# A four-stage graph network: the first stage's edge network moved into the pass that sorts the edges

## The chip, the cores and the metric

One core of a Trainium2 chip runs the whole program in one launch. The metric is the device time of that launch in microseconds (us). The core has five engines with queues of their own: PE (TensorE, matrix products into PSUM), DVE (VectorE), ACT (ScalarE), POOL (GpSimd, here mostly the issuer of indirect transfers) and SP (SyncE, issuer of plain transfers). ACT's queue issues some transfers too. Each queue is worked off in order, and semaphores join them.

## What is computed

There are 6250 nodes with 48 features (H) and 200000 edges with ends src and dst, sorted by dst. Each edge has 40 numbers for the first stage (`edge_attr_40`, RBF = 40), 16 for the second and a distance (`edge_weight`). Four graph stages follow one another, each with a residual and a layer norm. Only the first part of the first stage is touched by the change:

```python
gate = jax.nn.silu(edge_attr @ F1W + F1b) @ F2W + F2b          # 40 -> 48 -> 48, per edge
ei, ej = emb[atom_z[src]], emb[atom_z[dst]]
gate = gate + (ei * (ej @ adapt)).sum(-1, keepdims=True)       # one number per edge (G = 32)
cw = jnp.where(distances < CUT, 0.5 * (jnp.cos(jnp.pi * distances / CUT) + 1.0), 0.0)
mj = node_mult[dst]
msg = gate * h[dst] * (cw * mj)[:, None]
agg = segment_sum(msg, src); tot = clip(segment_sum(mj, src), 1e-08)
h = _ln(h + agg / tot[:, None], gn, bn)
for i in range(4):                                             # attention layers
    score = (qi * kj).sum(-1) + 0.1 * (edge_attr * qi[:, :40]).sum(-1) + logm[dst]
    ...
```

The later stages (an edge network with sums by dst, and two weighted sums) are the same in both kernels.

## The kernel before

**Layout.** The edges are padded to 200192 = 128 partitions x J columns, J = 1564; partition p holds 1564 consecutive edges. Work on edges goes by groups of columns. Sums over the edges of a node are made by sorting the edges by that node and running a segmented scan (DVE) along each partition.

**Counting, 0 to 535 us.** To sort by src, the kernel finds the place of each edge. `counted` (L311) builds one-hot tiles of the low and the high digit of src per column on DVE (`one_hots`, L304 and L307) and multiplies them on PE into a histogram of 128 x 49 counts, in NS = 4 streams (L317: column b goes to stream b mod 4). `places` adds up the streams. Beside this, `early` (L628 on) runs small steps between the columns: a search for where each dst begins, `node_table` (a row of 81 numbers per node: 48 features times multiplicity, 32 numbers of the type, the multiplicity), the scatter of these rows into `seed` at the first edge of each dst, and products of weights.

**The scatter pass, 535 to 3150 us.** It goes by chunks of CS = 16 columns, 98 of them. Four pieces of code are interleaved by the loop at the end of `sort`, which the tile framework then schedules:

- `ranked` (L366) gives the place `pos` of every edge, 8 columns at a time. Per 4 columns, ACT copies the running counts from PSUM (`hs_ps`) to `hs` (L385), PE looks the counts up (`g`, L387) and adds the 4 columns to `hs_ps` (L389), and only then can the next copy run. DVE makes the one-hot tiles (L304, L307, L380), compares the edges within a column (L395) and picks the result (L398, L400).
- `payload` (L415) loads 16 columns of the edges' attributes and copies them with src, dst and distance into a row tile `r_s` (three buffers), on ACT (L422 to L425).
- `expanded` (L660) fills the last 81 numbers of each row from `seed`: a load, then three slices of 27 features, each with a copy to PSUM on ACT (`run_v`, L287), a scan on DVE (`xf`, L270) and a copy into `r_s` on ACT (L676).
- `beside` does the same as `payload` for the rows that stay sorted by dst (`r_d`), clears tables and scatters a node table.

The main loop has POOL scatter each column of `r_s` to its place in `rows_s` (L172): 1564 indirect transfers, each of 128 rows of WS = 124 numbers (496 bytes). The program runs `ranked` four groups and `payload` one chunk ahead of the scatters.

**The gated sums, 3150 to 4347 us.** `gated_sums` reads the sorted rows back in groups of 40 columns. Per group, `begun` loads the rows `r` and the src-side type rows `q`, works out the cutoff on 128x40 tiles (L915 to L923, with a Sine on ACT, L920), multiplies the 48 features by it on POOL (L924), spreads q along the segments (L287, L270), forms the one number per edge that the types add to the gate (L931, L933) and writes `ra` (the 40 attributes and that number) to `rows_a`. The network itself is a skewed chain over four pairs of columns at a time: PE transposes `ra` (L954), ACT copies (L956), PE multiplies by F1W (L963; two extra rows carry the added number through), ACT applies Silu (L965), DVE copies the two extra rows (L966), PE multiplies by F2W (L973), and DVE multiplies by the features (`v`, L975). Then DVE scans the 49 sums (L986), ACT transposes them into `st` (L989) and writes them out.

**After that.** `between` joins the sums to the nodes (to 4505 us). The four attention layers (to 14060 us) read `rows_a` per 40 columns and gather 40 rows per group on POOL. The edge network (to 17180 us) and the two weighted passes (to 21800 us) follow.

Of the kernel before, what the change touches and what calls it, by code (L numbers as in the profile page):

```python
# [19 lines left out]
P = 128  # L20
N, E, H = 6250, 200000, 48
NB = 49
# [23 lines left out]
def gnn_kernel(ctx: ExitStack, tc: tile.TileContext, A, out: bass.AP):  # L46
# [78 lines left out]
    RA = RBF + 1  # L125
    f1w = const.tile([2 * RA, 2 * H + 2], F32, name="f1w")
    V.memset(f1w, 0.0)
    f1b = const.tile([2 * H, 1], F32, name="f1b")
    f2 = const.tile([2 * H + 3, 2, H], F32, name="f2")
    V.memset(f2, 0.0)  # L130
    for t in range(2):
        nc.sync.dma_start(f1w[t * RA:t * RA + RBF, t * H:(t + 1) * H], A["L0_gnn_F1W"])
        nc.sync.dma_start(f1w[t * RA + RBF:(t + 1) * RA, 2 * H + t:2 * H + t + 1], ones_pp[0:1, 0:1])
        nc.sync.dma_start(f1b[t * H:(t + 1) * H, :], A["L0_gnn_F1b"].rearrange("(w o) -> w o", o=1))
        nc.sync.dma_start(f2[t * H:(t + 1) * H, t, :], A["L0_gnn_F2W"])
        nc.sync.dma_start(f2[2 * H + t:2 * H + t + 1, t, :], ones_pp[0:1, 0:H])
        nc.sync.dma_start(f2[2 * H + 2:2 * H + 3, t, :], A["L0_gnn_F2b"].rearrange("(o w) -> o w", o=1))
# [4 lines left out]

    W0 = H + G + 1
    WS, WD = 3 + RBF + W0, 3 + EF
    rows_a = dram.tile([EP, RA], F32, name="rows_a")
# [153 lines left out]
    NS = 4  # L299
# [11 lines left out]
    def counted(pool, hist, rows_, lo, hi, ns, B):  # L311

        for j0 in range(0, J, B):
            n = min(B, J - j0)
            ol, oh = one_hots(pool, rows_, lo, hi, j0, n, B)
            for b in range(n):
                T.matmul(hist[:, b % ns, :NB], ol[:, b, :], oh[:, b, :],  # L317
                         start=(j0 + b < ns), stop=(j0 + b >= J - ns))
            yield

    def places(k, pool, psum, hist, ns, bases):

        of = pool.tile([P, ns, NB], F32, name="of")
        V.tensor_copy(of, hist[:, :, :NB])
# [41 lines left out]
    def ranked(k, pool, big, psum, consts, lo, hi, key, keyrow, lorow, bases, pos):  # L366

        B = 8
        hs_ps = psum.tile([P, NS, NB], F32, name="hs_ps", bufs=1)
        T.matmul(hs_ps, ident, bases, start=True, stop=True)  # L370
        for j0 in range(0, J, B):
# [11 lines left out]
            for b0 in range(0, n, NS):  # L383
                hs = big.tile([P, NS, NB], F32, name="hs")
                tc.keep_in_program_order(S.copy(hs, hs_ps[:, :, :NB]))  # L385
                for b in range(NS):
                    T.matmul(g[:, b0 + b, :], olt[:, b0 + b, :], hs[:, b, :], start=True, stop=True)  # L387
                for b in range(NS):
                    T.matmul(hs_ps[:, b, :NB], ol[:, b0 + b, :], oh[:, b0 + b, :], start=False, stop=True,  # L389
                             skip_group_check=True)  # L390
# [6 lines left out]
            pick = big.tile([P, B, NB], F32, name="pick")[:, :n, :]  # L397
# [17 lines left out]
    def payload(pool, k, j0, attr, ends, ew):  # L415
# [3 lines left out]
        a = by_columns(pool, wid, attr.shape[1], f"a_{k}", CS)  # L419
        tc.keep_in_program_order(nc.sync.dma_start(a, pj(attr)[:, s, :]))  # L420
        r = by_columns(pool, wid, rows[k].shape[1], f"r_{k}", CS, bufs=3)
        tc.keep_in_program_order(S.copy(r[:, :, 3:3 + attr.shape[1]], a))  # L422
        S.copy(r[:, :, 0], ends[k][:, s])
        S.copy(r[:, :, 1], ends["d" if k == "s" else "s"][:, s])
        S.copy(r[:, :, 2], ew[:, s])  # L425
        return r

    def sort(k, attr, ends, ew, early=None, behind=None, more=None, beside=None):
# [3 lines left out]
        with tc.tile_pool(name=f"sort_{k}", bufs=1) as sp:  # L432
# [3 lines left out]
            with tc.tile_pool(name=f"sort_hist_{k}", bufs=1) as hp, \  # L436
# [13 lines left out]
                hist = psum.tile([P, NS, 512], F32, name="hist")  # L450
# [17 lines left out]
            with tc.tile_pool(name=f"sort_io_{k}", bufs=2) as io, \  # L468
# [7 lines left out]
                rest = more(io, psum2) if more else lambda j0, r: None  # L476
# [21 lines left out]
    fall_i = ends_pool.tile([P, 1], I32, name="fall_i")  # L498
    nsd = ends_pool.tile([P, J], F32, name="nsd")
    logm = const.tile([P, NB], F32, name="logm")  # L500
    t0 = ends_pool.tile([P, NB, W0], F32, name="t0")
# [82 lines left out]
    def node_table(pool, psum):  # L584
# [5 lines left out]
        nc.sync.dma_start(both[:, 0], A["L0_gnn_emb"])  # L590
# [8 lines left out]
        for b0 in range(0, NB, 7):  # L599
            yield  # L600
            z = pool.tile([P, 7, P], I32, name="types", bufs=2)
            nc.sync.dma_start(z, bass.AP(tensor=types.tensor, offset=types.offset + b0 * P, ap=[[0, P], [1, 7 * P]]))
# [24 lines left out]

    def early(pool, hp, psum):  # L628
# [8 lines left out]
        for _ in range(22):  # L637
            yield
        next(search)
        yield from node_table(hp, psum)  # L640
        for _ in range(18):
            yield
# [3 lines left out]
        weight_products(psum)  # L646

# [12 lines left out]
    def expanded(pool, psum):  # L660

        fac = factors(pool, "fac", SG, CS)
# [702 lines left out]
```

## Time and profile before

| | us |
|---|---|
| runs | 21802.45, 21820.60, 21820.88; median 21820.6 |
| profiled execution | 21803.16, of which the span is 21801.4 |
| busy in the span: PE, DVE, ACT, POOL | 5648.7, 8101.9, 4776.3, 13861.4 |
| mean granted TensorE clock | 0.621 of full speed |

One execution was profiled; times of single instructions come from it. In the profile's groups a line reads: source line, engine, operation, output<-inputs, shapes, count | busy us, mean ns of one | idle time of the engine just before these instructions, and what released it. In the timeline a line reads: start, duration, engine, source line, operation, with the idle time before it and its releaser in brackets. "issue" is time in which the engine waited for nothing that the profile shows; "remote" is a release whose source the profile can't name.

### The profile page before, as it was taken

What the parts mean: (1) busy time and instruction counts of PE and PEld (TensorE: products, weight loads), DVE (VectorE), ACT (ScalarE), POOL (GpSimd) and SP (SyncE); (2) the same over time, 40 slices, a digit from 0 to 9 for tenths busy, and PEclk for the clock granted to TensorE, in tenths of its full rate; (3) what the DMA queues carried; (4) which work ended last, traced back from release to release, by engine and by line L of the source; (5) the groups of instructions that cost most, each with busy time, mean ns of one, the idle gap of its engine ahead of it and who ended that gap; (6) DMA issues with size and microseconds to landing.
All of it is one profiled execution on the core that took longest, in us unless ns stands there. A gap on an engine that the chain in (4) does not pass through costs nothing.

```text
span 21801.4 us, 86436 instructions
## 1 busy us (share of the span) xinstructions
PE 5648.7 (26%) x19138; PEld 3381.8 (16%) x19138; DVE 8101.9 (37%) x16477; ACT 4776.3 (22%) x6603; POOL 13861.4 (64%) x13410
## 2 busy tenths in 40 slices
PE   2332337622222222222222222244544200000000
PEld 2332334410001000110001000133333100000000
DVE  6554557743343434333433343322222211110001
ACT  0332334411111111111111111133333200001111
POOL 2566651177776777677776777644444577777777
PEclk9999995555555555555555555566666655555555
DMA  5455444422222222232222222211111111111111
GB/s 156 160 168 135 163 165 180 168 79 86 85 88 65 88 85 88 65 88 85 88 82 70 86 88 86 59 41 43 43 45 44 34 36 34 36 36 36 36 36 36
DMA packets 873557, 1792.31 MB, mean 82 GB/s; under 512 B 365490, under 2 KB 546658, under 8 KB 868034
## 3 DMA queue, kind: packets, MB, share of 16 engines
q1 hardware_dynamic: 349038, 860.63, 12.1%
q0 software_dynamic: 427520, 547.67, 10.9%
q10 hardware_dynamic: 96468, 378.32, 4.6%
q8 instruction: 163, 2.67, 0.1%
q14 instruction: 368, 3.01, 0.0%
HBM read 1144.48 MB, written 641.17 MB: 82 GB/s over the span
## 4 chain that ended last, share of the span: by engine, by line
POOL 29%; issue 13%; PE 6%; another core or an unknown queue 4%; DVE 3%; ACT 2%; DMA 0%; ACTq 0%; POOLq 0%; DVEq 0%; SPq 0%
POOL t L167 28%; PE ps L1216 2%; PE ps L1223 2%; PE ps L1231 2%; POOL own L167 1%; PE ps_t L1209 1%; ACT run_v L287 1%; ACT st L1239 1%; DVE qf L270 1%; DVE sf L270 1%; DVE run_v L268 0%; DVE q L1134 0%; DMA t<-tab_x,other 0%; ACT at L1211 0%
## 5 line engine op out<-in xcount | busy, mean ns | idle before, releaser
L167 POOL DMA_INDIRECT t<-tab_kv,other x6256 | 6586.8, 1053 | 2117.7 <-issue 2075.2
L167 POOL DMA_INDIRECT t<-tab_x,other x4692 | 4787.2, 1020 | 2619.5 <-issue 1459.6
L1132 PE MATMUL ka<-t,ident 128*128 128x480 f32 (+2 forms) x1264 | 1209.1, 1060 | 6818.1 <-DMA t<-tab_kv,other 5869.4
L172 POOL DMA_INDIRECT rows_s<-r_s,scratch x1564 | 1524.8, 975 | 1032.8 <-ACT r_s L422 528.6
L1134 DVE TENSOR_TENSOR q<-qf,ka 128x480 f32<-128x480 f32 (+2 forms) x632 | 676.6, 1074 | 3791.7 <-issue 3146.9
L1132 PEld LDWEIGHTS ka<-t,ident 128*128 128x128 f32 x1264 | 316.8, 310 | 7533.7 <-issue 4066.5
L270 DVE TENSOR_TENSOR_SCAN qf<-fac,run_v 128x480 f32<-128x480 f32 (+1 forms) x943 | 1028.8, 1092 | 672.1 <-DVE run_v L268 357.1
L841 PE MATMUL cy_ps<-ident,last_s 128*48 128x128 f32 (+1 forms) x4 | 1.6, 405 | 4524.6 <-DVE last_s L276 4524.6
L1164 ACT COPY st<-m 128x40 f32<-128x40 f32 (+3 forms) x164 | 42.8, 261 | 4895.8 <-DVE sc L1137 3754.0
L387 PE MATMUL g<-hs,olt 128*128 128x49 f32 x3128 | 758.7, 417 | 1323.0 <-ACT hs L385 764.4
L287 ACT COPY run_v<-q 128x480 f32<-128x480 f32 (+1 forms) x943 | 851.8, 916 | 707.7 <-DMA q<-spread_s 258.6
L1133 PE MATMUL ka<-r,tenth 128*128 128x400 f32 (+2 forms) x1264 | 954.6, 858 | 0.0
L1225 DVE TENSOR_SCALAR h<-ps,b 128x512 f32<-128x512 f32 x391 | 293.6, 751 | 1710.6 <-PE ps L1216 902.9
L387 PEld LDWEIGHTS g<-hs,olt 128*128 128x128 f32 x3128 | 695.9, 327 | 1375.5 <-ACT hs L385 791.9
L1313 DVE TENSOR_TENSOR run_v<-t,w_ps 128x480 f32<-128x480 f32 (+3 forms) x164 | 142.1, 912 | 1832.9 <-DMA t<-tab_x,other 1832.9
L268 DVE SCALAR_TENSOR_TENSOR run_v<-last_s,ns,run_v 128x12 f32<-128x12 f32 x480 | 98.0, 219 | 1935.4 <-issue 1680.1
L924 POOL TENSOR_TENSOR r<-r,u 128x1920 f32<-128x1920 f32 (+3 forms) x41 | 135.5, 3305 | 1037.0 <-DVE u L923 958.7
L270 DVE TENSOR_TENSOR_SCAN sf<-dec,run_v 128x480 f32<-128x480 f32 (+5 forms) x820 | 731.3, 922 | 122.3 <-remote 57.1
L841 PEld LDWEIGHTS cy_ps<-ident,last_s 128*48 128x48 f32 (+1 forms) x4 | 0.5, 127 | 4525.3 <-ACT st L1319 2261.5
L1216 PE MATMUL ps<-at,w 112*128 112x512 f32 x782 | 535.7, 774 | 496.2 <-ACT h L1218 471.7
L1163 ACT COPY st<-sf 128x1960 f32<-128x1960 f32 (+3 forms) x164 | 621.1, 3787 | 44.9 <-DVE sf L270 25.1
L1156 DVE TENSOR_TENSOR run_v<-t,es 128x480 f32<-128x480 f32 (+2 forms) x656 | 616.7, 962 | 13.9 <-DVE sf L270 5.3
(395 smaller groups left out, 14775.8 us busy)
## 6 DMA issues: line engine op xcount, KB each, us to landing
q<-spread_s SPq DMA_DIRECT2D x190, 960.0 KB
state_a<-st ACTq DMA_DIRECT2D x152, 1000.0 KB
r<-rows_a SPq DMA_DIRECT2D x152, 820.0 KB
state_h<-st ACTq DMA_DIRECT2D x114, 960.0 KB
t<-tab_kv,other POOLq DMA_INDIRECT x6256
r<-rows_s SPq DMA_DIRECT2D x38, 2480.0 KB
t<-tab_x,other POOLq DMA_INDIRECT x4692
seed<-zeros SPq DMA_DIRECT2D x17, 3726.0 KB
```

Source lines behind the costliest of these rows:

```text
L167: return nc.gpsimd.indirect_dma_start(out=dst, out_offset=None, in_=table, in_offset=bass.IndirectOffsetOnAxis(ap=idx, axis=0))
L172: i = nc.gpsimd.indirect_dma_start(out=table, out_offset=bass.IndirectOffsetOnAxis(ap=idx, axis=0), in_=src, in_offset=None)
L270: V.tensor_tensor_scan(flat[:, f0 * wid:(f0 + n) * wid], fac[:, :n * wid], v.rearrange("p f c -> p (f c)")[:, :n * wid], 0.0, OP.mult, OP.add)
L287: return lambda v, f0, n: S.copy(v, by_feature(src[:, :, f0:f0 + n]))
L387: T.matmul(g[:, b0 + b, :], olt[:, b0 + b, :], hs[:, b, :], start=True, stop=True)
L1132: T.matmul(ka, ident, t[:, j0:j1, 0:H], start=True, stop=False)
L1133: T.matmul(ka[:, :, 0:RBF], tenth, r[:, j0:j1, 0:RBF], start=False, stop=True)
L1134: V.tensor_mul(q[:, j0:j1, :], by_column(qf)[:, j0:j1, :], ka)
L1156: V.tensor_mul(v, by_feature(t[:, :, H + 1 + f0:H + 1 + f0 + n]), es[:, None, :].to_broadcast([P, n, wid]))
L1163: S.copy(st[:, :, 0:H + 1], by_column(sf))
L1216: T.matmul(ps, w1, at, start=True, stop=True)
L1223: T.matmul(ps, w2, h1, start=True, stop=True)
```

## The change

- A second, transposed copy of `edge_attr_40` (`edge_attr_40_t`: 80 rows, two columns' attributes, by 782 x 128) becomes an input. From it, per 16-column chunk, the first layer and Silu run in the scatter pass a chunk ahead (`hidden`, in four tiles `hid0` to `hid3`), and the second layer runs when the chunk's rows are filled; ACT copies its result from PSUM into `r_s`.
- A row of `rows_s` grows from 124 to 172 numbers (688 bytes): attributes first, then src, dst, the cutoff in place of the distance, 48 gate numbers, and the 81 from `seed`.
- NS goes from 4 to 8: `hs` is copied once per 8 columns. `hist` takes one PSUM bank, and its streams start from a zero product.
- `cutoff` works out all 128x1564 cutoffs once, at the end of `early`. `node_table` moves ahead in `early`, with its loads on ACT's queue.
- In the gated sums the network, the transposes, the cutoff and POOL's product are gone. Groups have 32 columns. The number that the types add is multiplied by the cutoff, and one ACT operation per column joins it to the gate: gate x cutoff + number. The sums go through PSUM by `runs`.
- `rows_a` has 40 numbers; the first attention layer reads the attributes from `rows_s` and writes `rows_a` for the other three.
- Buffers: `r_d` two, `a_s`, `a_d`, `seeds`, `hs`, `pick` and `at_e` one.

```diff
-    f1w = const.tile([2 * RA, 2 * H + 2], F32, name="f1w")
+    f1w = const.tile([2 * RBF, 2 * H], F32, name="f1w")
-    f2 = const.tile([2 * H + 3, 2, H], F32, name="f2")
+    f2 = const.tile([2 * H + 1, 2, H], F32, name="f2")
-    WS, WD = 3 + RBF + W0, 3 + EF
-    rows_a = dram.tile([EP, RA], F32, name="rows_a")
+    WS, WD = RBF + 3 + H + W0, 3 + EF
+    rows_a = dram.tile([EP, RBF], F32, name="rows_a")
-    NS = 4
+    NS = 8
...
     def ranked(...):
-            for b0 in range(0, n, NS):
-                hs = big.tile([P, NS, NB], F32, name="hs")
-                tc.keep_in_program_order(S.copy(hs, hs_ps[:, :, :NB]))
-                for b in range(NS):
-                    T.matmul(g[:, b0 + b, :], olt[:, b0 + b, :], hs[:, b, :], start=True, stop=True)
-                for b in range(NS):
-                    T.matmul(hs_ps[:, b, :NB], ol[:, b0 + b, :], oh[:, b0 + b, :], start=False, stop=True,
-                             skip_group_check=True)
+            hs = big.tile([P, NS, NB], F32, name="hs", bufs=1)
+            tc.keep_in_program_order(S.copy(hs, hs_ps))
+            for b in range(n):
+                T.matmul(g[:, b, :], olt[:, b, :], hs[:, b, :], start=True, stop=True)
+            for b in range(n):
+                T.matmul(hs_ps[:, b, :], ol[:, b, :], oh[:, b, :], start=False, stop=True, skip_group_check=True)
...
     def payload(...):
-        a = by_columns(pool, wid, attr.shape[1], f"a_{k}", CS)
+        a = by_columns(pool, wid, attr.shape[1], f"a_{k}", CS, bufs=1)
-        r = by_columns(pool, wid, rows[k].shape[1], f"r_{k}", CS, bufs=3)
+        r = by_columns(pool, wid, rows[k].shape[1], f"r_{k}", CS, bufs=3 if k == "s" else 2)
...
+    def cutoff(pool):
+        n = pool.tile([P, J], F32, name="n_cut")
+        V.tensor_scalar(cw, ew, 1.0 / (2.0 * CUT), None, op0=OP.mult)
+        V.tensor_scalar(n, cw, ROUND, None, op0=OP.add)
+        V.tensor_scalar(n, n, -ROUND, None, op0=OP.add)
+        V.tensor_sub(cw, cw, n)
+        S.activation(cw, cw, AF.Sin, scale=math.pi)
+        V.tensor_mul(cw, cw, cw)
+        V.tensor_scalar(cw, cw, -1.0, 1.0, op0=OP.mult, op1=OP.add)
+        V.scalar_tensor_tensor(cw, ew, CUT, cw, op0=OP.is_lt, op1=OP.mult)
...
-    def expanded(pool, psum):
+    def expanded(pool, psum, net_psum):
+        hid = [pool.tile([2 * H + 1, 4, P], F32, name=f"hid{i}", bufs=1) for i in range(4)]
...
+        def hidden(j0):
+            wid = min(CS, J - j0)
+            at = pool.tile([2 * RBF, CS // 2, P], F32, name="at_e", bufs=1)[:, :wid // 2, :]
+            tc.keep_in_program_order(nc.sync.dma_start(at, A["edge_attr_40_t"][:, j0 // 2:(j0 + wid) // 2, :]))
+            for k0, n, hi in parts(j0):
+                ps = net_psum.tile([2 * H, 4, P], F32, name="ps_1")[:, :n]
+                T.matmul(ps, f1w, at[:, k0:k0 + n], start=True, stop=True)
+                S.activation(hi[0:2 * H], ps, AF.Silu, bias=f1b)
+        hidden(0)
...
         def rest(j0, r):
+            for k0, n, hi in parts(j0):
+                ps = net_psum.tile([P, 4, 2, H], F32, name="ps_2")[:, :n]
+                for k in range(n):
+                    T.matmul(ps[:, k], hi[:, k, :], f2, start=True, stop=True)
+                S.copy(r[:, 2 * k0:2 * (k0 + n), RBF + 3:RBF + 3 + H], ps.rearrange("p k t w -> p (k t) w"))
+            if j0 + CS < J:
+                hidden(j0 + CS)
...
     def gated_sums(ep, psum):
...
+        def gates(c):
+            r = by_columns(ep, wid, WS - RBF, "r", C0, bufs=3)
+            nc.sync.dma_start(r, pj(rows["s"][:])[:, s, RBF:])
...
+            V.tensor_mul(q[:, :, :G], by_column(qf), r[:, :, B0:B0 + G])
+            pair = ep.tile([P, C0], F32, name="pair")[:, :wid]
+            V.tensor_reduce(pair, q[:, :, :G], AX.X, OP.add)
+            V.tensor_mul(pair, pair, r[:, :, 2])
+            for j in range(wid):
+                S.activation(r[:, j, N0:X0], r[:, j, N0:X0], AF.Identity, bias=pair[:, j:j + 1], scale=r[:, j, 2:3])
+            return r, fac, first
+        def sums(c, r, fac, first):
+            def values(v, f0, n):
+                if f0 == H:
+                    S.copy(v, by_feature(r[:, :, WS - RBF - 1:]))
+                else:
+                    V.tensor_mul(v, by_feature(r[:, :, N0 + f0:N0 + f0 + n]), by_feature(r[:, :, X0 + f0:X0 + f0 + n]))
+            sf = by_features(ep, H + 1, wid, "sf", C0, bufs=1)
+            runs(psum, sf, fac, first, before["s"], H + 1, values, cols=C0)
...
+        ahead = gates(0)
+        for c in range(len(parts)):
+            now = ahead
+            if c + 1 < len(parts):
+                ahead = gates(c + 1)
+            sums(c, *now)
...
-                r = by_columns(ep, wid, RA, "r")
-                nc.sync.dma_start(r, pj(rows_a[:])[:, s, :])
+                r = by_columns(ep, wid, RBF, "r")
+                if l == 0:
+                    nc.sync.dma_start(r, pj(rows["s"][:])[:, s, 0:RBF])
+                    nc.scalar.dma_start(pj(rows_a[:])[:, s, :], r)
+                else:
+                    nc.sync.dma_start(r, pj(rows_a[:])[:, s, :])
```

## Prediction

> **What bounds the kernel now.** I read the windows by stage first, because the mean shares (POOL 64%) mix stages with different limits. Columns: length, then busy time and count of PE, weight loads, DVE, ACT, POOL, the clock, DMA share, GB/s.
>
> ```profile
> 0.00:535.00 535.00, 122.44 (x1724) 108.72 (x1725) 361.32 (x329) 16.71 (x56) 141.98 (x157) 1.00 0.53 155
> 535.00:3150.00 2615.00, 848.03 (x4688) 785.66 (x4687) 1436.73 (x4888) 827.81 (x1854) 1570.61 (x1612) 1.00 0.50 156
> 3150.00:4347.00 1197.00, 816.49 (x2742) 556.11 (x2742) 892.22 (x1497) 584.27 (x723) 137.92 (x45) 0.60 0.44 176
> ```
>
> The change touches three stages: counting (535 us), the scatter pass (2615 us), the gated sums (1197 us). No engine is above 60% in the scatter pass, nor above 75% in the gated sums: both are bound by chains of hand-offs, so busy time moved between them is worth little; what counts is where it stands in the chain. The waits and groups of the scatter pass come next (waited for: us, times, longest; then busy, mean ns, idle before):
>
> ```profile
> ACT hs L385 <- remote: 1123.5, 164, 32.1
> POOL rows_s L172 <- ACT r_s L422: 528.6, 81, 19.1
> L387 PE MATMUL g<-hs,olt 128*128 128x49 f32 x3128 | 758.7, 417 | 1323.0 <-ACT hs L385 764.4 <-issue 557.4 <-ACT run_v L287 1.0
> ```
>
> POOL waits 6.5 us on average, 81 times in 98 chunks, for the last copy into the row tile r_s. The timeline shows why:
>
> ```profile
> 1027.90 0.96 POOL L172 DMA_INDIRECT rows_s<-r_s,scratch  x1 [0.30 <-issue]
> 1034.20 0.96 POOL L172 DMA_INDIRECT rows_s<-r_s,scratch  x1 [5.34 <-ACT r_s L422]
> 1035.46 1.07 POOL L172 DMA_INDIRECT rows_s<-r_s,scratch  x1 [0.30 <-issue]
> ...
> 1024.51 0.33 PE L389 MATMUL hs_ps<-oh,ol 128*128 128x49 bf16 x4 [1.07 <-issue]
> ...
> 1031.83 0.32 ACT L385 COPY hs<-hs_ps 128x196 f32<-128x196 f32 x1 [7.96 <-remote]
> 1032.05 0.41 ACT L422 COPY r_d<-a_d 128x256 f32<-128x256 f32 x1
> 1032.36 0.93 ACT L676 COPY r_s<-xf 128x432 f32<-128x432 f32 x1
> 1033.18 0.74 ACT L422 COPY r_s<-a_s 128x640 f32<-128x640 f32 x1
> 1034.35 0.32 ACT L385 COPY hs<-hs_ps 128x196 f32<-128x196 f32 x1 [0.43 <-PE hs_ps L389]
> ```
>
> The counts' matmuls end at 1024.84, but the copy of hs that needs them starts only at 1031.83, 2.97 us after the chunk's last scatter ended (1028.86). Everything behind that copy in ACT's queue is held with it, the r_s copies among it, and the next burst starts 2.37 us after the release. The next copy of hs follows 2.52 us on, promptly. What delays the signal the trace does not name ("remote"). So a chunk is 16 scatters (pitch 0.96 + 0.30, or 1.265 us: 20.24 us) plus a gap of some 4.8 us: 25.0 us. 98 of these are 2450 us, and about 165 us are disturbed chunks.
>
> **The change, part by part.** The profiled execution took 21803.2 us, of which the span is 21801.4; the median of the runs is 17 us higher. A measurement of this kernel tells about 0.2% (44 us) from no change.
>
> *Scatter pass, work added.* Each 16-column chunk gets 2 first-layer matmuls, 2 Silu, 8 second-layer matmuls and 2 copies from PSUM into r_s. Prices come from the gated sums (granted clock 0.60; ahead of 3200 us the profile has no record of it, and its 1.00 there says nothing):
>
> ```profile
> L973 PE MATMUL ps<-f,hid 99*128 99x96 f32 x1564 | 380.1, 424 | 136.1 <-DVE hid L966 135.9
> L963 PE MATMUL ps<-at,f1w 82*98 82x512 f32 x390 | 341.7, 975 | 11.5 <-ACT at L956 11.5
> L965 ACT ACTIVATE hid<-ps,f1b 96x512 f32<-96x512 f32 x195 | 132.7, 681 | 55.9 <-PE ps L963 41.0 <-ACT v L945 8.2 <-DVE ra L933 3.4
> ```
>
> PE: 341.7/195 = 1.75 and 380.1/195 = 1.95 us a part, two parts: 7.4 us on top of 848.0/98 = 8.65, or 16 of 20.24 at least. ACT: 2 x 0.68 for Silu, 2 x about 0.75 for copies of 128x384 (the 128x320 copy took 0.707, the 128x480 one 0.973), less the saving on hs (four 0.322 become two of about 0.5, since 128x405 took 0.530): 8.4 becomes some 10.7 us. DVE stays at 14.7. No engine reaches the 20.24 us of scatters. A scatter of 192-byte rows (spread_s) took 959 ns and one of 496-byte rows 975, so 688-byte rows should cost POOL about 985: +16 us in all at most. DMA carries 0.72 MB more on 4.0 MB a chunk: its share of 0.50 becomes 0.6 to 0.73. By these rows POOL's scatters cover all of it: zero by itself, and without that cover PE's 7.4 us would be the price.
>
> *Scatter pass, hand-offs.* In eight streams the ACT-to-PE rounds through hs fall from four a chunk to two, each about twice 2.52 less a copy's fixed part: 4.8 us. But there are four new PE-to-ACT hand-offs a chunk (two Silu, two copies of ps_2), all in ACT's one queue, and the first-layer PSUM tile has a single buffer, so PE in turn waits for Silu. By the order of the two programs, behind the copy of hs that ended last there now stand: r_d's copies, a_s's, the first writes of the next r_s, in every other turn the next chunk's ps_2 copy, and then the last xf copy that completes r_s. At pitches from the timeline (0.42 for hs, 0.31 and 0.11 for r_d, 0.65 for a_s, three to five small ones at 0.11, 0.45 for ps_2 where it stands there, 0.93 for xf) that is 2.8 to 3.4 us, against 2.37 now. Two outcomes bound the price:
> - The late signal stays, once a chunk: the period grows by 0.4 to 1.05 us, +40 to +105 us over 98 chunks, and more where one of the new hand-offs is late too. In parts of the pass the two rounds may end before the burst is far on (a release followed by 2 x 4.8 us reaches the fifth or so scatter, and the trace has prompt copies up to there), which would take some gaps away. Bounds 0 to +250; I take +110, just above the counted work, because four waits come and two go.
> - No signal is late on the path: 20.6 to 23.5 us a chunk, 2185 to 2470 us for the stage with the disturbed chunks: -430 to -145.
>
> *Gated sums.* This stage loses all its PE work, eight small DVE operations and a Sine a part, and POOL's 3457 ns product of 128x1920. It gains one ACT operation per column, 1564 of 128x48 with scale and bias read from tiles. Its parts shrink from 40 columns to 32 (50 instead of 41). By the order of the changed program ACT and DVE alternate: the 32 activations follow DVE's pair sums; behind them stand a small copy (0.14), two copies of run_v (128x384, 0.71 by pitch), the transposing copy st (3.935 x 1568/1960 = 3.15), fac (0.48); then DVE's scans of q, product, reduction (2.625 and 1.485 at 40 columns, 2.1 and 1.2 at 32) and two slices of the sums that stand between them, 8.9 us. So a part is 32p + 14.1 us, p being the pitch of one activation. DVE's own work (some 17 us) and the load of r lie beside it.
>
> ```profile
> L945 ACT COPY v<-r 128x40 f32<-128x40 f32 x38 | 9.8, 258 | 0.0
> L956 ACT COPY at<-ps_t 82x512 f32<-82x512 f32 x195 | 112.8, 578 | 253.4 <-PE ps_t L954 252.5 <-ACT v L945 0.7
> ```
>
> No row has both operands from a tile. Silu (bias from a tile, 681) beside this copy of the same width (578) prices one at 0.10 us: 0.26 + 0.21 = 0.47 long, less the 0.11 by which neighbouring small ACT operations overlap (220 ns long, issued every 0.105): p = 0.35, nearest to the rows, and 25.3 us a part. 48 of these and 45 us for the ends: 1260, +65. If tile operands cost nothing, p = 0.14: 18.6 us, 938, -260. If nothing overlaps, p = 0.47: 29.1 us, 1444, +245.
>
> The Trainium skill's page "ScalarE: Activation LUTs", section *What ACT_TABLE_LOAD costs*, speaks against many small activations: 186 ns fixed, 0.833 ns an element, about 93 ns for each pointer operand, neighbours overlapping by about 93. By it alone p would be 0.32 (an estimate from that page), and this term +15 instead of +65. No trace here shows an activation with two.
>
> *Counting.* cutoff() on 128x1564 is seven DVE operations between 1.03 us (row L533) and 1.78 (row L523), a Sine and a table load of 1.28: about 12 us behind the last hist matmul or just ahead of it. Four more streams add some ten DVE operations of 0.2 us. The node table starts earlier, and its loads go to ACT's queue, which has room (16.7 us busy). DVE's 361.3 of 535 hides part: -10 to +30, I take +12.
>
> *First attention layer.* It reads r in pieces of 160 bytes from the wider rows and writes rows_a, 820 KB a chunk, on ACT's queue. A chunk is 57 us of gathers on POOL with DMA at 0.28, which covers both; without that cover 41 chunks would lose perhaps 1 us each: 0 to +40, I take +10.
>
> Sum for the likeliest: 21803 + 110 + 65 + 12 + 10 = 22000; with half of the 17 us to the median, 22010. Its own range: 21860 to 22330.
>
> **Rivals.**
> - *The hand-offs become prompt* (faster). Place: the gap ahead of each chunk's first scatter. If halving the rounds lets ACT run a chunk ahead (r_s has three buffers), POOL issues without gaps. Price: -430 to -145 there, with the other terms (+87) a total of 21460 to 21745, about 21600 at its middle. It decides where r_s(c+1) is complete before the burst of chunk c ends. For it: no engine but POOL is busy for more than 16 of 20.24 us. Against it: the copy of hs above came late deep in a burst, and without gaps the whole pass is one burst.
> - *The new hand-offs stick too* (still slower). If a Silu or a ps_2 copy also waits for the end of a burst, the gap holds two rounds: 20.24 + 2.7 + 5 to 8.5 us, 28 to 31.5 a chunk, +300 to +640; total 22200 to 22530. For it: four waits on PE are added to ACT's queue. Against it: the network runs a chunk ahead.
> - *Cheap activations* (p near 0.14) over an unchanged scatter pass: -260 + 110 + 22, total about 21675.
>
> **How the numbers follow.** Likeliest case 0.42, prompt hand-offs 0.33, sticking ones 0.18, cheap activations 0.07. The likeliest is slower but for an edge (0.05) within 44 us of no change; prompt hand-offs are faster but for 0.02 that end within it. Faster: 0.31 + 0.07 - 0.01 = 0.37; same 0.05 + 0.02 - 0.01 = 0.06; slower: 0.37 + 0.18 + 0.02 for activations at their dear end = 0.57. The range takes the prompt case down to 21400 and the sticking one up to 22550.
>
> **What would show it right or wrong.** Right: POOL's wait for r_s still comes once a chunk, at 25.5 to 26.5 us, with a hs copy released some 2.7 us after the last scatter; the activations stand 0.35 us apart and the gated sums last about 1260 us. Wrong: bursts that follow each other at 1.265 us without a gap (prompt), a Silu or ps_2 copy with a long "remote" idle (sticking), activations under 0.2 us apart, or a stage behind 4500 us that has moved by more than 50.

## The result and the profile after

The changed kernel takes 22092.4 us (median of 4 runs, 22085.1 to 22109.4) against 21813.4 for the kernel before on the same chip: a ratio of 1.0135, 95% interval 1.0123 to 1.0148. The profiled execution of the changed kernel has a span of 22091.2 us; the prediction was 22010, slower.

The chips that the runs were taken on matter here. The result and experiments e10 to e12 come from chips on which the kernel before takes 21690 to 21815 us; e1 to e9 come from two others on which it takes 18668. Ratios are always against the kernel before on the same chip.

By stage, in us of the profiled executions (counting: to the start of the first scatter into `rows_s`; pass: from there to the start of the last of these; sums: from there to the first scatter of the joined sums into `spread_s`, so some 80 us of `between` are in it):

| | counting | pass | sums | rest | span |
|---|---|---|---|---|---|
| before | 561.0 | 2589.5 | 1278.0 | 17372.9 | 21801.4 |
| after | 564.8 | 2914.3 | 1243.4 | 17368.7 | 22091.2 |
| difference | +3.8 | +324.8 | -34.6 | -4.2 | +289.8 |

So all of the loss is in the scatter pass. The prediction counted the gated sums without `between`, to the first gather of the node sums: by that end they take 1164.6 us after (3479.0 to 4643.6), where it gave 1197 for before. The windows by stage of the changed kernel, with the columns as in the prediction:

```profile
0.00:564.80 564.80, 156.05 (x1851) 133.80 (x1852) 395.47 (x422) 32.92 (x80) 146.96 (x158) 1.00 0.53 156
564.80:3479.00 2914.20, 1475.40 (x6520) 1173.05 (x6519) 1400.30 (x4815) 982.15 (x2031) 1591.77 (x1612) 1.00 0.52 163
3479.00:4722.40 1243.40, 14.34 (x50) 9.57 (x50) 717.69 (x1520) 774.53 (x1893) 50.40 (x53) 1.00 0.52 152
```

PE has taken on the network (1475 us busy in the pass), and it is still busy for only half of the stage; POOL, the floor, is at 55%. The time is in waits (us, times, longest), here of the scatter pass of the changed kernel:

```profile
POOL rows_s L171 <- ACT r_s L714: 842.4, 77, 38.5
PEld g L385 <- ACT hs L383: 837.7, 126, 28.6
PE g L385 <- ACT hs L383: 767.8, 126, 28.4
DVE pick L395 <- remote: 654.9, 51, 30.0
ACT r_s L706 <- remote: 649.6, 42, 29.0
ACT hs L383 <- remote: 482.5, 71, 17.5
```

POOL's wait for the rows has grown from 528.6 to 842.4 us, and "remote", the signal from PE that comes late, now holds two more instructions than the copy of hs: DVE's pick and, the new one, ACT's copy of the network's result into r_s (L706). A part of the timeline shows the worst form, which comes back once in five chunks, and the next long gap:

```profile
1000.81 0.97 POOL L171 DMA_INDIRECT rows_s<-r_s,scratch  x1 [0.30 <-issue]
1021.31 1.14 POOL L171 DMA_INDIRECT rows_s<-r_s,scratch  x1 [19.53 <-ACT r_s L714]
...
979.55 0.54 PE L387 MATMUL hs_ps<-oh,ol 128*128 128x49 bf16 x8
1007.10 3.65 PE L385 MATMUL g<-hs,olt 128*128 128x49 f32 x16 [27.00 <-ACT hs L383]
...
1006.18 0.48 ACT L706 COPY r_s<-ps 128x384 f32<-128x384 f32 x1 [27.46 <-remote]
1020.12 0.92 ACT L714 COPY r_s<-xf 128x432 f32<-128x432 f32 x1
...
1069.11 0.49 ACT L383 COPY hs<-hs_ps 128x392 f32<-128x392 f32 x1 [16.03 <-remote]
1085.01 0.97 POOL L171 DMA_INDIRECT rows_s<-r_s,scratch  x1 [16.98 <-ACT r_s L714]
```

PE's matmuls end at 980.1, just ahead of a second burst that follows the first without a gap (its first scatter is at 981.6). Their consumers are released at 1004.7 to 1006.2, 2.9 to 4.4 us after the last scatter of the *second* burst (1001.8). Only then do two rounds of counts and the network's hand-offs run, and the next burst starts 19.5 us late, 16.6 us after the first release. The other long gap of the five follows one burst alone: a copy of hs is released at 1069.1, 1.1 us after that burst's last scatter (1068.0), and the next burst starts 15.9 us later. Over the pass the periods of chunks repeat in fives: 24.5, 21.2, 39.7, 26.4, 38.0 us, 30.0 on average, where the kernel before has mostly 25.0. Two clears fall on each five chunks.

### The profile page after: what moved, and what is told of

It reads as the page before. It is cut to its first block, busy times and chain, and to the rows that moved or that the text cites. A ratio compares the mean times of both kernels' runs of the same rounds, so it can differ in the third digit from the quotient of the medians.

```text
span 22091.2 us, 86171 instructions
## 1 busy us (share of the span) xinstructions
PE 5498.3 (25%) x18358; PEld 3241.0 (15%) x18358; DVE 7893.4 (36%) x16431; ACT 5126.1 (23%) x7944; POOL 13775.5 (62%) x13369
## 5 line engine op out<-in xcount | busy, mean ns | idle before, releaser
L166 POOL DMA_INDIRECT t<-tab_kv,other x6256 | 6600.2, 1055 | 2104.7 <-issue 2069.2
L171 POOL DMA_INDIRECT rows_s<-r_s,scratch x1564 | 1544.9, 988 | 1343.6 <-ACT r_s L714 842.4
L269 DVE TENSOR_TENSOR_SCAN qf<-fac,run_v 128x480 f32<-128x480 f32 (+6 forms) x970 | 1027.9, 1065 | 801.1 <-DVE run_v L267 388.4
L286 ACT COPY run_v<-q 128x480 f32<-128x480 f32 (+6 forms) x970 | 851.0, 893 | 620.5 <-DMA q<-spread_s 262.4
L385 PE MATMUL g<-hs,olt 128*128 128x49 f32 x3128 | 713.0, 415 | 996.6 <-ACT hs L383 768.4
L267 DVE SCALAR_TENSOR_TENSOR run_v<-last_s,ns,run_v 128x12 f32<-128x12 f32 (+1 forms) x725 | 151.2, 219 | 2206.6 <-issue 1583.1
L269 DVE TENSOR_TENSOR_SCAN sf<-fac,run_v 128x480 f32<-128x480 f32 (+6 forms) x742 | 729.1, 994 | 80.4 <-issue 57.0
```

The costliest lines, as they stand in the source:

```text
L166: return nc.gpsimd.indirect_dma_start(out=dst, out_offset=None, in_=table, in_offset=bass.IndirectOffsetOnAxis(ap=idx, axis=0))
L171: i = nc.gpsimd.indirect_dma_start(out=table, out_offset=bass.IndirectOffsetOnAxis(ap=idx, axis=0), in_=src, in_offset=None)
L267: V.scalar_tensor_tensor(v[:, :n, 0], before_[:, f0:f0 + n], first, v[:, :n, 0], op0=OP.mult, op1=OP.add)
L269: V.tensor_tensor_scan(flat[:, f0 * wid:(f0 + n) * wid], fac[:, :n * wid], v.rearrange("p f c -> p (f c)")[:, :n * wid], 0.0, OP.mult, OP.add)
L286: return lambda v, f0, n: S.copy(v, by_feature(src[:, :, f0:f0 + n]))
L385: T.matmul(g[:, b, :], olt[:, b, :], hs[:, b, :], start=True, stop=True)
```

## The experiments

**e1: the network left out of the scatter pass.** The rows stay wide and the copies stay.

```diff
-                ps = net_psum.tile([P, 4, 2, H], F32, name="ps_2")[:, :n]
-                for k in range(n):
-                    T.matmul(ps[:, k], hi[:, k, :], f2, start=True, stop=True)
-                S.copy(r[:, ...], ps...)
-            if j0 + CS < J:
-                hidden(j0 + CS)
+                S.copy(r[:, ...], ps2[:, :n]...)      # ps2: zeros, set once
```

> The changed kernel without the network in the scatter pass: the 4 first-layer and second-layer matmul groups, Silu and the load of the transposed attributes are left out, and ACT's two copies a chunk into the rows take zeros from a PSUM tile, so the rows are as wide and as many copies are made. Theory A (the new hand-offs between PE and ACT stand in ACT's one queue behind late PE signals and cost the scatter pass its 325 us): the pass falls back to about 2600 us, the time to 21740 to 21830. Rival B (wider rows and more DMA load cost it): the pass stays above 2800 us, the time at 22000 or more. Rival C (the eight-column count rounds cost it): likewise no fall, with copies of hs still held until the burst's end.

Measured: 18672.4 us against 18667.9, ratio 1.0003 (0.9994 to 1.0013). On the chip of this run the pass is quite another: 2103 us, chunks mostly of 20.4 to 21.1, no gap ahead of them. It can't decide between A, B and C, since on such a chip there is little to be lost (the whole changed kernel's pass takes 2116 there, in e5); e11 repeats it where there is.

**e2: the eight streams alone, in the kernel before.**

```diff
-    NS = 4
+    NS = 8      # with hist and the rounds of ranked() as in the change
```

> The kernel before with the counts in eight streams and nothing else (hs and pick with one buffer). Theory A: one copy of hs a chunk is still held until some 2.7 us after the last scatter, so the chunk stays near 25 us and the time within 60 us of before. Rival C (eight-column rounds are themselves dearer, 4.8 us each against 2.5): a chunk of 26 us or more, 21900 or more. If halved rounds free the path, the chunk falls to 21 to 23 us and the time to 21450 to 21650.

Measured: 18656.6, ratio 0.9995 (0.9985 to 1.0004), no change. The pass is bound by POOL (chunks mostly of 20.2 to 20.9 us, pass 2087), so fewer rounds have nothing to gain.

**e3: the cutoff once, alone, in the kernel before.**

```diff
-        S.copy(r[:, :, 2], ew[:, s])
+        S.copy(r[:, :, 2], (cw if k == "s" else ew)[:, s])
...
-            u = ... n = ... S.activation(u, u, AF.Sin, scale=math.pi) ...      # in begun()
-                                    u[:, :, None].to_broadcast([P, wid, H]),
+                                    r[:, :, 2:3].to_broadcast([P, wid, H]),
```

> The kernel before with the cutoff worked out once ahead of the scatter pass and carried in the rows, POOL's product kept in the gated sums; a_s and a_d have one buffer and r_d two, to make room. Theory: some 5 us more in the counting, 1.2 to 2 us less in each of 41 groups of the gated sums (eight small DVE operations and a Sine leave the chain): -40 to -80 us, 21735 to 21775. Rival: these operations lay beside other work, no change within 20 us. If single-buffered attribute loads matter, the scatter pass is longer by 50 us or more.

Measured: 18649.5, ratio 0.9990 (0.9981 to 1.0000): -18 us, which by the total is the rival's case (no change within 20 us). By stage, with e2 for the kernel before, which has no profile on such a chip: the sums are at 1244 against 1274, -30 instead of -40 to -80, and the counting is at 430 against 415. So the stage did get shorter, by less than expected, and half of it is given back ahead of the pass.

**e4: the dst-side clears moved out of the pass.**

```diff
-            yield from cleared(spread["d"], nc.sync)
...
+                if l == 1 and c < 17:
+                    nc.scalar.dma_start(view_d[:, c], zeros[:, None, :23 * H].to_broadcast([P, 4, 23 * H]))
```

> The changed kernel with the 17 clears of the dst-side spread table (2.2 MB each) moved out of the second half of the scatter pass into the second attention layer, on ACT's queue. Theory D (each clear in the scatter pass upsets the rhythm of chunks, 26.4 us undisturbed, and costs about 9 us): the second half runs at 26.4 us a chunk, -130 to -170 us, time 21920 to 21960. Rival: the uneven rhythm (24.5, 21.2, 39.7, 26.4, 38.0 us) comes of the late signals alone: no change within 40 us.

Measured: 18811.8, ratio 1.0078 (1.0061 to 1.0094). The edit did not do what it says: nothing tied the clears to the second layer, and the scheduler put all 17 into the counting (3 to 264 us), which took 543 us instead of the 458 of e5. The clears did leave the pass, and the pass is not shorter for it: 2148 us, against 2116 in e5. On this chip signals are prompt; on chips where they are late the run says nothing on theory D.

**e5: the changed kernel again.**

> The changed kernel as it is, run beside the kernel before on whatever chip this is: the runs above were taken on a chip on which the kernel before takes 18668 us and no PE signal of the scatter pass is late. Theory A (the loss comes from late PE signals): where signals are prompt, the scatter pass is bound by the scatters at 20.3 to 21 us a chunk and the changed kernel is within 60 us of before; where they are late, +0.9 to 1.6%. Rival B (wider rows, more work): +1.3% on either chip.

Measured: 18698.1 against 18668.8, ratio 1.0016 (1.0006 to 1.0025). Theory A, and B falls: the same kernel costs 0.16% here and 1.35% there. The waits of the scatter pass on this chip:

```profile
POOL rows_s L171 <- issue: 407.3, 1337, 0.3
DVE run_v L267 <- ACT run_v L286: 366.5, 119, 25.6
ACT hid L690 <- PE ps L689: 325.7, 145, 5.5
```

POOL waits for nothing but its own issue, "remote" is not among the large waits, and chunks mostly take 20.4 to 21.5 us. The trace's semaphore events say the same: of PE's signals in the pass that were recorded, 1 of 750 came over 1 us after the matmul's modelled end, against some 230 to 250 of 648 in the changed kernel's profile where it takes 22091 (by how closely record and end are matched), 71 of them over 10 us. In the kernel before the figure there is 177 of 396, and in e2 1 of 384. Of the 92 that are over 5 us late in the kernel before, 71 come in a gap behind a burst, half of them 2.6 to 2.9 us after the end of its last scatter. Only PE's are so late: of the signals of ACT and DVE in the profiles of the kernel before and the changed kernel there, none is 5 us late. Since a matmul's end is modelled, this does not tell a late signal from a matmul that ended late.

**e6: the gate joined by POOL.**

```diff
-            for j in range(wid):
-                S.activation(r[:, j, N0:X0], r[:, j, N0:X0], AF.Identity, bias=pair[:, j:j + 1], scale=r[:, j, 2:3])
+            gate = r[:, :, N0:X0]
+            nc.gpsimd.tensor_tensor(gate, gate, r[:, :, 2:3].to_broadcast([P, wid, H]), op=OP.mult)
+            nc.gpsimd.tensor_tensor(gate, gate, pair[:, :, None].to_broadcast([P, wid, H]), op=OP.add)
```

> The changed kernel with the 32 small ACT operations a group replaced by two POOL operations over the whole group (gate times cutoff, plus pair). Theory: in the gated sums 32 activations of 0.32 us pitch (10.3 us) stand in the chain of ACT and DVE; two POOL products of 128x1536 (2.8 us each, from 3.46 us for 128x1920) take their place: about 4.5 us less in each of 50 groups, -200 to -250 us against the changed kernel. Rival: the activations lie beside DVE's scans, or POOL and DVE slow one another: less than 60 us either way.

Measured: 18422.8, ratio 0.9867 (0.9851 to 0.9884), 275 us less than e5 (-200 to -250 were expected), of which the sums are 255 (1238.5 to 983.6) and the pass 17: a scatter takes 960 ns there and 971 in e5, which the last section comes back to. The activations did stand in the chain. POOL and DVE did slow one another, as the rival said, without undoing the gain: DVE's products of 128x384 take 1479 ns beside POOL's instead of 829 in e5. In its window of the sums DVE is now the nearest to a bound:

```profile
2558.00:3541.00 983.00, 14.29 (x50) 9.57 (x50) 851.76 (x1519) 287.39 (x328) 403.42 (x152) 1.00 0.68 193
```

**e7: the clears tied to the second layer,** by a source tile of that layer.

```diff
-            yield from cleared(spread["d"], nc.sync)
...
+                none = ep.tile([P, 4 * H], F32, name="none", bufs=1)
...
+                    nc.sync.dma_start(view_d[:, c], none[:, None, :].to_broadcast([P, 23, 4 * H]))
```

> The changed kernel with the 17 clears of the dst-side spread table taken out of the scatter pass and tied to the second attention layer by a source tile of that layer (the earlier try let them slip into the counting, which grew by some 100 us). Theory D (clears upset the chunks): where PE signals are late, -120 to -170 us against the changed kernel; where they are prompt, -20 to -60. Rival (clears are hidden): no change within 20 us.

Measured: 18730.4, ratio 1.0033 (1.0020 to 1.0045): 32 us *more* than e5. The pass went from 2116 to 2147, as in e4, its chunks without clears taking about 21.5 us instead of 20.8. Neither theory expected that. Between 1950 and 2560 us POOL waits for the rows again (for ACT's L714 28 times, 41.4 us in all, against once for 0.3 us in e5), and ACT waits for the loads of `seeds` (69.6 us, against 25.3); why these loads come later without the clears is open.

**e8: a pause in the burst.**

```diff
+                    if j % CS == 7:
+                        for _ in range(12):
+                            nc.gpsimd.memset(pause, 0.0)
```

> The changed kernel with twelve small POOL fills (128x128) after the eighth scatter of each chunk, so that the burst of 16 has a pause of 1.5 to 4 us in its middle. Theory A (a PE signal that comes deep in a burst is released only where POOL stops issuing): on a chip with late signals they are released in the pause, the longest chunks (38 to 40 us) vanish, and the scatter pass is shorter in spite of the pause, 2500 to 2800 us. Rival (release has nothing to do with POOL): each chunk is longer by the pause, +150 to +400 us. On a chip with prompt signals: + the pause, about 98 times 1.5 to 4 us.

Measured, one run: 18987.7. All 1176 fills were scheduled between 420 and 1454 us, so most of them into the first two fifths of the pass, several sets to a chunk, and the chip has prompt signals: the pass is longer by the fills (2405 us). Inconclusive. That POOL's bursts hold PE's signals is still read from the traces only.

**e9: three POOL products.** As e6, and POOL multiplies the gate by the features; ACT copies the product into the sums' PSUM tiles.

```diff
+            nc.gpsimd.tensor_tensor(gate, gate, r[:, :, X0:X0 + H], op=OP.mult)
...
-                    V.tensor_mul(v, by_feature(r[:, :, N0 + f0:N0 + f0 + n]), by_feature(r[:, :, X0 + f0:X0 + f0 + n]))
+                    S.copy(v, by_feature(r[:, :, N0 + f0:N0 + f0 + n]))
```

> The changed kernel with the gate joined by POOL as in the run before last, and POOL also multiplies the joined gate by the features (a third product of 128x1536); ACT then copies the product into the sums' PSUM tiles in place of DVE's five products a group. Theory: with the gate on POOL, DVE's work (851 of 981 us in the gated sums) sets the pace; taking 285 us of it to POOL and ACT, which are busy for 403 and 287, shortens the stage by 100 to 200 us more: 18220 to 18320 where the kernel before takes 18668 (0.976 to 0.981). Rival: POOL's longer chain (three products of 3.2 to 3.9 us behind the pair sums) takes DVE's place: no gain over 0.987. On a chip where the kernel before takes some 21800, late PE signals add their 330 us to the scatter pass, and the ratio is 0.99 to 1.0.

Measured: 18357.6, ratio 0.9833 (0.9816 to 0.9851). The sums fell by 67 us more, to 916.4, less than the 100 to 200 expected.

**e10: the kernel before again,** for its profile.

> The kernel before as it is, for its profile where PE signals are prompt. Theory A: no copy of hs is held to the end of a burst; the scatter pass goes at 20.3 to 20.8 us a chunk (2085 to 2100 us) against 2116 of the changed kernel, the counting takes 10 to 40 us less than the changed kernel's 458, and the gated sums 1270 to 1280 against 1239; the sum of these differences is the measured +29 us. Rival: the gaps ahead of the chunks are there too (2450 us or more), and what is shorter lies elsewhere.

Measured: 21812.4 (21815.5 beside it). This chip has late signals, so there is no profile of the kernel before where they are prompt; with e2 in its place, e5 has +43 in the counting, +29 in the pass and -36 in the sums, against 41.5 between their medians. What e10 does show is that the gaps are the kernel's on such a chip and not of one run: chunks of 25.0 to 25.4 with a few of 35, and some 170 of 380 PE signals late.

**e11 and e12: on a chip with late signals.** e11 is e1 with e9's sums, e12 is e7 with e9's sums.

> The changed kernel with two edits in stages that do not overlap: the network left out of the scatter pass as in the first experiment (matmuls, Silu and their load are left out, the two copies a chunk take zeros), and the sums with three POOL products. Meant for a chip with late PE signals (the kernel before takes some 21810 there, 2578 to 2590 in the scatter pass). Theory A (the network's own hand-offs carry the loss): the scatter pass falls from 2914 to 2500 to 2620 us. Rival C (the eight-column rounds or the wider rows carry it): 2800 us or more. On a chip with prompt signals it is 2100 either way, and the time 18330 to 18350.

> The changed kernel with the dst-side clears in the second attention layer and the sums with three POOL products, a candidate for a version faster than both. On a chip with late PE signals, theory D (a clear upsets the rhythm by about 9 us): the second half of the scatter pass goes at the undisturbed 26.4 us a chunk, the pass at 2740 to 2800 us, the gated sums at about 920, the time 21580 to 21680, below the kernel before. Rival: the long chunks of 38 to 40 us stay without clears: 2880 us or more. On a chip with prompt signals, 18380 to 18400.

Measured: e11 21405.0 against 21689.1 (0.9865, 0.9846 to 0.9884); e12 21561.8 (0.9943, 0.9923 to 0.9962).

| | counting | pass | sums |
|---|---|---|---|
| e11 | 550.1 | 2585.0 | 920.1 |
| e12 | 560.1 | 2753.1 | 921.3 |

e11: without the network the pass takes 2585 us, as in the kernel before (2578 to 2590, on other chips), though it has the eight-column rounds, the wide rows and the two more copies. So these cost nothing together that can be seen, and the network (its load, matmuls, Silu and hand-offs) carries the 325 us but for some 20: a scatter takes 974 ns in the changed kernel and 960 in e11 and e12, 14 ns for 1564 of them, and that comes with the other edit (see the last section). The copy of hs is still the late one in e11, as in the kernel before:

```profile
ACT hs L383 <- remote: 975.6, 79, 27.2
...
POOL rows_s L171 <- ACT r_s L710: 469.4, 71, 15.1
```

e12: in its first half, with the src-side clears, the cycle of 24.4, 21.2, 39.6, 26.2 and 36 to 38 us is the changed kernel's; in its second half, without clears, nearly all chunks take 26.2 to 26.3 us. Theory D: on such a chip a clear upsets the rhythm. The pass is 161 us shorter than the changed kernel's; 150 of these lie in the last 45 chunk periods, some 10 of them by the shorter scatters, so a clear cost 8 to 9 us. It takes both, the network and the clears. On the chip of e11 and e12, the first 42 periods, which have clears in both, take 1080 us without the network and 1218 with it. The last 45 take 1157 with clears and no network (e11), 1176 with the network and no clears (e12), and 1327 with both (the changed kernel, on the chip of the result). Whether a clear acts by its 2.2 MB of transfers or by its place in SP's queue is not shown. Two consecutive bursts of the second half, first scatter and the copy released ahead of it:

```profile
2435.55 0.49 ACT L383 COPY hs<-hs_ps 128x392 f32<-128x392 f32 x1 [3.65 <-remote]
...
2438.92 0.96 POOL L171 DMA_INDIRECT rows_s<-r_s,scratch  x1 [6.08 <-ACT r_s L714]
2465.13 0.96 POOL L171 DMA_INDIRECT rows_s<-r_s,scratch  x1 [6.07 <-ACT r_s L714]
```

The gap is 6.1 us instead of 4.8, and the burst starts 3.37 us after the release instead of 2.37: the likeliest case of the prediction as it was written down.

e12 and e9 are faster than both kernels on the kind of chip where each ran (0.9943 and 0.9833). All of that comes of the sums, some 357 us shorter than before (for e9, than in e2); the counting and the pass give part of it back.

## Why the prediction was right, and where its terms were off

**The bound.** That the scatter pass hangs on a chain of hand-offs, with late PE signals and the r_s copies behind them, held, and so did the sign. It holds on chips where PE's signals come late, which the trace of before could not say. But more than one signal a chunk is late: a sign that the prediction set down for being wrong, a Silu or ps_2 copy with a long "remote" idle, did come (ps_2 42 times, up to 29.0 us; Silu 21 times, up to 31.6).

**Scatter pass, the steady chunk.** The prediction had 2.8 to 3.4 us from release to burst and a period of 25.5 to 26.5. Measured: 3.37 us (e12) and 26.4 us (26.2 in e12) in the chunks that no clear disturbs. 1.4 us times 98 is 137, against the +110 taken; some 25 of these 137 are the longer scatters (974 ns against 958).

**Scatter pass, the disturbed chunks: the step that failed.** "About 165 us are disturbed chunks" was carried over unchanged. (26 of the 165 lie ahead of the first scatter, since the window began at 535.) What the pass has beyond 98 steady chunks is 2589 - 98 x 25.0 = 139 us before (first to last scatter) and 2914 - 98 x 26.4 = 327 after: +188 that the sum did not have. Some 80 to 90 us of either are the ten chunk periods about the scatters of the node table (337 us before, 345 after), and these did carry over; what grew is the chunks with the clears. e12 shows that the clears set it off, and e11 that it takes the network. The likeliest mechanism, argued from the timeline: a disturbance lets two bursts join, PE's signals then wait through both, and ACT holds not one round but several behind them, which is why both long gaps have some 16 us from release to burst. The rival "the new hand-offs stick too" described that chunk on the mean (28 to 31.5 us; the mean is 29.9, and a ps_2 copy waits 27.5 us in the lines above), so this stage ended in the rival's price range. Of the five periods of the cycle only 26.4 lies in the likeliest case's range.

**Gated sums.** The activations stand (10.28 - 0.41)/31 = 0.318 us apart, not 0.35:

```profile
3989.96 10.28 ACT L957 ACTIVATE r<-r,pair 128x48 f32<-128x48 f32 x32 [7.70 <-DVE pair L955]
4000.15 0.19 ACT L965 COPY run_v<-r 128x32 f32<-128x32 f32 x1
4000.29 1.52 ACT L286 COPY run_v<-q 128x384 f32<-128x384 f32 x2
4001.75 2.83 ACT L973 COPY st<-sf 128x1568 f32<-128x1568 f32 x1
4004.49 0.49 ACT L253 COPY fac<-ns 128x372 f32<-128x372 f32 x1
4005.27 0.60 ACT L286 COPY run_v<-q 128x256 f32<-128x256 f32 x1 [0.29 <-ACT fac L253]
4013.28 2.98 ACT L957 ACTIVATE r<-r,pair 128x48 f32<-128x48 f32 x9 [7.41 <-DVE pair L955]
```

One activation alone lasts 0.412, against the 0.47 that I had from the row pair, so two tile operands cost less; neighbours overlap by 0.09, not 0.11. The Trainium skill's page "ScalarE: Activation LUTs", section *What ACT_TABLE_LOAD costs*, gave an estimate of 0.32, as worked out in the prediction, and the trace agrees with it. A part takes 4013.28 - 3989.96 = 23.3 us, so the rest of the chain is 13.0 instead of 14.1 us: st took 2.83, not 3.15, as it is not proportional to its length, and from fac to the next activations it is 8.0, not 8.9. 50 parts of 2 us less are 100 us: -35 instead of +65, and 1165 us by the prediction's own end of the stage instead of 1260. The order of the chain was as predicted, and e6 confirms that the activations stand on it.

**Counting and first layer.** +3.8 instead of +12, within its bounds. The first layer, from its first gather to the second layer's, takes 2407.7 us against 2407.1: +0.6 instead of +10, at the low end of its bounds; all that follows the sums is 4 us shorter. Where signals are prompt the counting does grow (458 in e5, 415 in e2).

**The sum.** +110 + 65 + 12 + 10 against +325 - 35 + 4 - 4. Two terms that were off by 215 and 100 in opposite directions left the total 80 us from the forecast. That it came so near is luck; either error alone would still have left the total in the range. A slip without effect: by its own prices ACT's 8.4 us a chunk become 11.0, not 10.7; 10.0 were measured (982.15/98).

**The other rivals.** Prompt hand-offs: not on this chip; and on a chip that has them the kernel before takes 18668 us and an edit of it (e2) has them too, so nothing is gained: passes of 2087 (e2) and 2116 us (e5) are both POOL's scatters. The prediction took promptness for something that the change could bring. Cheap activations: no.

## What to carry to other kernels

Where a chain of hand-offs sets the period, an engine's idle time is not room: the network's 7.4 us of PE a chunk fitted easily by busy time, and the late signals around it cost some 300 us. When work is moved into such a stage, price what disturbs the stage now again with the new chain behind it, and do not carry it over. And price 32 small operations in a chain against one large one on an idle engine: two POOL operations in place of 32 activations gave 255 us, although DVE's products beside them took 1479 ns instead of 829.

## What the runs showed of the hardware

The same kernel differs by 17% between chips of one kind (21813 and 18668 us), and not evenly: the scatter pass is bound by late PE signals on the ones and by POOL on the others. With it goes the gather in the attention layers: its mean is 1052 to 1055 ns on the chips with late signals (median 948 to 949, with a fifth of them over 1100) and 944 where signals are prompt. What follows the sums takes 17373 us on the one kind of chip (before) and 14883 on the other (e2), so most of the 17% lies there and not in the pass. PE's signals come within 0.12 us of the matmul's end in 749 of 750 cases on the one, and up to 30 us late on the other, most of the latest ones in the gap behind a POOL burst. The profiles with late signals also hold fewer semaphore records (14424 in the changed kernel's pass, against 45534 in e5). What delays the signals, and why only on some chips, is open.

Scatters differ between kernels, and hardly by their rows. A scatter into `rows_s` takes POOL 971 ns in e5 (688-byte rows) and 958 in e2 (496-byte rows), medians, 20 us over the pass and near the 16 that the prediction had for wider rows. But in e6, with the same 688-byte rows, it takes 960, and the scatters of 192-byte rows into `spread_s` differ in the same way:

```profile
L171 POOL DMA_INDIRECT rows_s<-r_s,scratch x1564: 967/971/1614, 458.3 to 2574.7; - x196
L171 POOL DMA_INDIRECT spread_s<-own,start_at_s x196: 965/969/1674, 3813.2 to 10350.5; - x196
...
L171 POOL DMA_INDIRECT rows_s<-r_s,scratch x1564: 954/960/1698, 458.3 to 2557.7; - x196
L171 POOL DMA_INDIRECT spread_s<-own,start_at_s x196: 952/958/1727, 3541.3 to 10078.0; - x196
```

(The first two lines are e5's, the others e6's; ns, minimum, median and longest.) So 192 bytes more a row cost 2 ns, and the other 11 come to every scatter of a kernel: they are there in the changed kernel, e1, e4, e5, e7 and e8, whose gated sums have no POOL product, and not in the kernel before, e2, e3, e6, e9, e11 and e12, which have one. Why is open.
